# Swapping which engine reads a shared PSUM bank first: the bias addition of VectorE ahead of ScalarE's copy

## The chip, the cores and the metric

The kernel runs on one core of a Trainium2 chip. The metric is the device time of one launch in microseconds (us); three launches of the kernel before gave 3203.61, 3207.11 and 3209.1 us, so the median is 3207.11 us. A profile comes from one more execution of the same program, which took 3203.72 us.

## The reference

The input is 64 graphs of 256 nodes with 256 features each, and one sparse adjacency matrix `adj` (256 x 256) shared by all. Four layers follow each other. Layers 0, 1 and 3 have the same form, and layer 2 is an attention layer:

```python
# layers 0, 1, 3
pre_u = h @ W1[:256]                 # per node
pre_v = h @ W1[256:]
hidden = relu(pre_u[:, None] + pre_v[None, :] + b1)
S   = sigmoid(hidden @ W2 + b2)      # per pair of nodes
a_t = einsum('buv,bud->bvd', S * adj, h)
m_t = (adj^T h) * h
z   = beta1*h + beta2*(a_t @ Wa + ba) + beta3*(m_t @ Wm + bm)
# layer 2
feats = h @ W1^T;  f1 = feats @ W2 + b2
vals  = softmax(leaky_relu(f1[:,None] + f1[None,:]) + adj) @ feats
out   = vals + bias2 + h
```

`S` only matters where `adj` is not zero, and the kernel computes scores for those pairs of nodes (edges) alone.

## The kernel before

All data is fp32. Two graphs at a time (`g` = 0, 1) go through the four layers as one state, and two such states, side "a" and side "b", run interleaved: while one state is in its score stage (`scores`, L768 on, the heavy part), the other does the light parts of its layers. Sixteen rounds of this cover the 64 graphs.

The order of instructions on TensorE, VectorE and ScalarE is written out by hand. `PLAN` (L65) holds one string of letters for each combination of layer and side; `beside` (L919) advances one generator per letter: `T` makes the scores of one block of edges (two selecting matmuls into a PSUM tile of pool `ga`, then two VectorE passes with accumulated sums), `F`, `O` and `R` do the same for edges that were gathered, for the diagonal and for the left-over edges, `L` and `N` advance the light state, and `E` and `Z` turn the sums into scores (`rated_all`, L791). All three engines take their instructions strictly in the order recorded. DMA queues of SyncE (SP) and GpSimd (POOL) are not part of that order; a scheduler places them by when their inputs are ready.

The function around the change is `before` (L726), a light part that runs at the start of layers 0, 1 and 3. For each half `m` of the nodes and each graph `g` (four times per layer) it does this:

- two accumulating matmuls write one PSUM tile `t` of 128 x 512 fp32: columns 0 to 255 are `pre_u` of 128 nodes and columns 256 to 511 are `pre_v`. The tile fills one bank. It comes from pool `ps`, which has four buffers.
- L748: ScalarE copies the first half of the bank to the SBUF tile `puv`.
- L749: VectorE adds the bias row `b1row` to the second half and writes it to `puv`.
- The two instructions read different halves of one bank. The framework orders any two engines that touch one bank, so the second of them in program order waits for the first.
- after the second graph of a half, two SP DMAs (L753) write `puv` to two tables in DRAM, `tableu` (ScalarE's half) and `tablev` (VectorE's half); `fetch` (L847) then gathers rows from them by indirect DMAs that POOL issues (L861).
- ScalarE rounds `puv` to the two `part` tiles (L762, two casts), and VectorE subtracts to get the remainders (L765). The `T` blocks of the next score stage read the parts.

`puv` has a single buffer, used by both states in turn. Copy and addition stand as pairs 384 times in a run.

Other ScalarE work that stands in its queue around these pairs, and that the prediction follows: `hwa` (L391, a copy that empties a `ga` tile), `h` (L462, a copy of transposed features), `hT` (L520 on), and in `rated_all` (L791 on) two activations that make `val` (tanh, then add 1). VectorE follows `val` with three tiny instructions on `wt` (L797 to L799) and with the product `rm` (L804), which TensorE multiplies with `gu`. `mT` (L378) is a VectorE product that TensorE needs for `Wm`. In layer 2 the pair `e` and `f` (L496, L499) already reads one bank with VectorE first and ScalarE second. Since helper `Noting` (L96) records every operation of the three engines, the profile puts them all on L104; the tiles' names tell them apart.

Of the kernel before, what the change touches and what calls it, by code (L numbers as in the profile page):

```python
# [12 lines left out]
ALU = mybir.AluOpType  # L13
# [33 lines left out]
def fetches_of(l):  # L47

    def part(b, x):
        y = 1 - x if places(b)[0] > places(b)[1] else x  # L50
        return b, x, y

    first, then = [], [(None, 0, 0)]
    for b in FETCHED[l]:
        one = [part(b, x) for x in range(2)]
        (first if min(places(b)) == 0 else then).append(one[0])
        (first if max(places(b)) == 0 else then).append(one[1])
    by = lambda p: p[1]
    first.sort(key=by)
    waiting = [p for p in then if p[0] and p[1] and min(places(p[0])) == 0]  # L60
    last = sorted((p for p in then if p[0] and p not in waiting), key=by)
    return [first, then[:1] + waiting + [(None, 1, 1)] + last]
# [25 lines left out]
def blk(c):  # L88
    return slice(c * P, (c + 1) * P)
# [37 lines left out]
def adj_seq_kernel(ctx: ExitStack, tc: tile.TileContext, a: dict, out: bass.AP):  # L127
# [15 lines left out]
    tensor, vector, scalar = Noting(nc.tensor), Noting(nc.vector), Noting(nc.scalar)  # L143
# [35 lines left out]
    w1, wa, wm, b1row, w2row, zbias = {}, {}, {}, {}, {}, {}  # L179
# [372 lines left out]
    def few(stack):  # L552
# [173 lines left out]
        def before(st, l):  # L726

            hT = st["hT"]
            st["puv"] = puv = one.tile([P, 2, 2, 2, D], FP, tag="puv", name="puv")
            st["parts"] = parts = [one.tile([P, 2, 2, 2 * D], FR, tag=f"part{k}" + st["side"], name=f"part{k}") for k in range(2)]  # L730
            order = [(m, g) for m in range(2) for g in range(2)]
            if l == LAST:
                order = [(m, g) for g in range(2) for m in range(2)]

            st["tables"] = [
                tables.tile([N, 2 * D], FP, tag="table" + t + st["side"], name="table" + t) for t in "uv"
            ]

            st["fetches"] = []
            st["fetched"] = {b: got_.tile([P, 2, D], FP, tag="fetched", name="fetched") for b in FETCHED[l]}  # L740
            st["left"] = one.tile([P, D], FP, tag="left" + st["side"], name="left")
            for m, g in order:
                if l == LAST and (m, g) == (1, 0):
                    st["flip"](1)
                t = psum()
                for c in range(2):
                    mm(out=t, lhsT=hT[:, c, g, blk(m)], rhs=w1[l][:, c], start=c == 0, stop=c == 1)
                scalar.copy(puv[:, m, 0, g, :], t[:, 0, :])  # L748
                vector.tensor_tensor(puv[:, m, 1, g, :], t[:, 1, :], b1row[l], ALU.add)  # L749
                if g == 1:  # L750
                    x = puv[:, m].rearrange("p w g d -> p (w g d)")
                    for w, rows in enumerate(st["tables"]):
                        nc.sync.dma_start(out=rows[blk(m)], in_=x[:, w * 2 * D : w * 2 * D + 2 * D])  # L753
                    st["fetches"] += fetches_of(l)[m]
                    if numbered:
                        fetch(st)
                    elif st not in unfetched:
                        unfetched.append(st)
                    yield
                    flat = [p[:, m].rearrange("p w d -> p (w d)") for p in parts]  # L760
                    for k, h in enumerate(halves):
                        scalar.copy(flat[k][h], x[h])  # L762
                    yield
                    for k, h in enumerate(halves):
                        vector.tensor_tensor(flat[k][halves[1 - k]], x[h], flat[k][h], ALU.subtract)  # L765
                yield
# [80 lines left out]
        def fetch(st):  # L847

            now, st["fetches"] = st["fetches"], []
            for block, x, y in now:  # L850
                rows, ids = st["tables"][y], (ids_u, ids_v)[y]
                if block is None:
                    to, ids = st["left"], (left_u, left_v)[x]
                    rows = rows.rearrange("n (g d) -> (n g) d", g=2)
                else:
                    f = SOME.index(block)
                    to, ids = st["fetched"][block].rearrange("p g d -> p (g d)"), ids[:, f : f + 1]
                    if places(block)[y] == 0:
                        rows = rows[blk(0)]
                with tc.issue_after(fetches[-1]) if fetches else nullcontext():  # L860
                    this = nc.gpsimd.indirect_dma_start(  # L861
                        out=to, out_offset=None, in_=rows, in_offset=bass.IndirectOffsetOnAxis(ap=ids, axis=0),
                        compute_op=(ALU.bypass, ALU.add)[x],
                    )
                fetches.append(this.ins)
# [26 lines left out]
        def stream(side, starts):  # L892

            sts = [{"b": b, "side": side} for b in starts]
            if side == "a":
                sts[0]["hT"] = hT0
            load(sts[0])
            short = dict(L=before(sts[0], GNN[0]))
            kind = None
            for i, st in enumerate(sts):  # L900
                yield short, kind, (st, GNN[0])
                yield dict(L=steps(after(st, GNN[0]), before(st, GNN[1])), N=turns(st)), (GNN[0], side), (st, GNN[1])
                yield dict(L=steps(after(st, GNN[1]), attention(st), before(st, GNN[2]))), (GNN[1], side), (st, GNN[2])
                short, kind = dict(L=after(st, GNN[2])), None
                if i + 1 < len(sts):
                    load(sts[i + 1])
                    short, kind = dict(L=after(st, GNN[2]), N=before(sts[i + 1], GNN[0])), (LAST, side)
            yield short, None, None
# [151 lines left out]
```

## Time and profile before

| | before |
|---|---|
| median of three launches | 3207.11 us (3203.61 to 3209.1) |
| profiled execution, device time | 3203.72 us |
| its span, first to last instruction | 3202.0 us |
| granted TensorE clock | 0.995 |
| one copy of the first half (ScalarE) | 372 ns, 384 times |
| one bias addition of the second half (VectorE) | 420 ns, 384 times |
| one cast to a part (ScalarE) | 1044 ns, 384 times |
| one subtraction (VectorE) | 1221 ns, 384 times |
| one `T` pass over 128 x 256 (VectorE) | 418 ns, 1920 times |

The span is the time from the first to the last instruction on the core; the device time is 1.7 us longer. "Busy" is the time in which an engine executes. A group of instructions is named by its output and inputs, `out<-in`, with partitions x elements; after the bar come its total time, the mean of one and the idle time of the engine right before such instructions, with what ended it after `<-`. In a timeline each row gives the start, the duration, the engine and the instruction, `xN` for N in a row, and in brackets the idle time before it. PE is TensorE, PEld its weight loads, DVE VectorE, ACT ScalarE.

### The profile page before, as it was taken

How to read it: one execution, taken by the hardware profiler on the slowest of the kernel's cores; microseconds unless marked ns; L12 is line 12 of the kernel's file. 1: busy time of each engine (PE TensorE's matmuls, PEld its weight loads, DVE VectorE, ACT ScalarE, POOL GpSimd, SP SyncE). 2: the span in 40 equal slices, each digit the busy share in tenths (PEclk: the TensorE clock that was granted, in tenths of full speed). 3: DMA queues.
4: the chain of work that ended last, by engine and by line, in shares of the span. 5: the costliest groups of instructions: out<-in, count | busy, mean ns of one | idle time of the engine just before them, and what ended most of it. 6: DMA issues, size and time to landing. Idle time of an engine off the chain costs nothing.

```text
span 3202.0 us, 48626 instructions
## 1 busy us (share of the span) xinstructions
PE 3117.7 (97%) x14648; PEld 2228.7 (70%) x14648; DVE 2913.5 (91%) x10312; ACT 1358.9 (42%) x2658; POOL 1875.4 (59%) x1371
## 2 busy tenths in 40 slices
PE   7999999999999999999999999999999999999998
PEld 4667777677767667676777776767767676676766
DVE  7989999898999989999899998989989899898998
ACT  3444444434344443434444444444443434434343
POOL 2747566564656647556475564756657465564754
PEclk8999999999999999999999999999999999999999
DMA  5757576675756758577576665757667576675755
GB/s 154 155 127 183 133 180 136 146 172 127 187 132 163 162 119 190 139 162 161 128 182 133 169 155 134 179 128 178 137 144 170 128 183 133 158 162 118 191 130 111
DMA packets 231726, 486.59 MB, mean 152 GB/s; under 512 B 30880, under 2 KB 48160, under 8 KB 231456
## 3 DMA queue, kind: packets, MB, share of 16 engines
q0 software_dynamic: 147456, 327.24, 51.8%
q1 hardware_dynamic: 82416, 154.96, 13.6%
q8 instruction: 119, 1.95, 0.3%
q10 hardware_dynamic: 1584, 1.20, 0.1%
q14 instruction: 151, 1.24, 0.1%
HBM read 365.84 MB, written 117.44 MB: 151 GB/s over the span
## 4 chain that ended last, share of the span: by engine, by line
PE 68%; DVE 17%; issue 4%; ACT 3%; DMA 3%; POOL 2%; DVEq 0%; POOLq 0%; ACTq 0%
PE ps L104 44%; PE ga L104 24%; DVE junk L104 6%; DVE part L104 5%; POOL fetched L861 2%; DVE rm L104 2%; DMA fetched<-tablev,ids_v 1%; DMA left<-tablev,left_v 1%; ACT logits L104 1%; ACT ro L104 1%; DVE e L104 1%; DVE mT L104 1%; DVE own L104 1%; DVE logits L104 1%; DVE puv L104 0%
## 5 line engine op out<-in xcount | busy, mean ns | idle before, releaser
L861 POOL DMA_INDIRECT fetched<-tableu,ids_u x576 | 739.0, 1283 | 880.8 <-DVE junk L104 272.9
L861 POOL DMA_INDIRECT fetched<-tablev,ids_v x576 | 877.1, 1523 | 333.8 <-DMA fetched<-tableu,ids_u 182.3
L104 PE MATMUL ps<-L_gnn_w,hT 128*128 128x512 f32 x1536 | 718.2, 599 | 9.4 <-issue 5.4
L104 DVE SCALAR_TENSOR_TENSOR junk<-ga,L_gnn_w2row 128x256 f32<-128x256 f32 x1920 | 713.8, 418 | 4.4 <-PE ga L104 1.5
L104 PE MATMUL ga<-part,pick_u 128*128 128x512 f32 x960 | 519.8, 542 | 6.0 <-DVE mT L104 3.3
L104 DVE TENSOR_TENSOR part<-puv,part 64x1024 fp32r<-64x1024 f32 x384 | 468.8, 1221 | 11.8
L104 ACT CAST part<-puv 64x1024 fp32r<-64x1024 f32 x384 | 401.0, 1044 | 164.6 <-DVE puv L104 155.5
L104 PEld LDWEIGHTS ps<-L_gnn_w,hT 128*128 128x128 f32 x1536 | 286.6, 191 | 263.2 <-issue 222.2
L104 DVE SCALAR_TENSOR_TENSOR junk<-fetched,L_gnn_w2row 128x256 f32<-128x256 f32 x1152 | 432.2, 420 | 17.7 <-DMA fetched<-tablev,ids_v 13.4
L104 PE MATMUL ga<-part,pick_v 128*128 128x512 f32 x960 | 380.0, 396 | 0.5 <-issue 0.4
L104 PE MATMUL ga<-L_gnn_Wa,hT 128*128 128x256 f32 x1536 | 366.5, 382 | 1.8 <-DVE junk L104 1.8
L104 PE MATMUL ga<-adj,h 128*128 128x256 f32 x1536 | 361.8, 380 | 0.1
L104 ACT COPY puv<-ps 128x256 f32<-128x256 f32 x384 | 139.7, 372 | 520.2 <-PE ps L104 394.6
L104 PEld LDWEIGHTS ga<-adj,h 128*128 128x128 f32 x1536 | 292.6, 191 | 75.8 <-issue 37.8
L104 PEld LDWEIGHTS ga<-L_gnn_Wa,hT 128*128 128x128 f32 x1536 | 291.5, 192 | 62.6 <-issue 23.3
L104 DVE TENSOR_TENSOR puv<-ps,L_gnn_b1row 128x256 f32<-128x256 f32 x384 | 156.2, 420 | 136.2 <-ACT puv L104 134.7
L104 PE MATMUL ps<-sa,hwa 128*128 128x256 f32 x1024 | 239.5, 382 | 2.2 <-DVE sa L104 1.7
L104 DVE TENSOR_TENSOR rm<-gva,val 128x1024 f32<-128x1024 f32 x192 | 234.6, 1222 | 3.5 <-ACT val L104 0.6
L104 PEld LDWEIGHTS ga<-part,pick_u 128*128 128x128 f32 x960 | 182.3, 190 | 78.1 <-issue 35.7
L104 PE MATMUL ps<-mT,L_gnn_Wm 128*128 128x512 f32 x512 | 235.9, 593 | 0.0
L104 ACT ACTIVATE ro<-gvo,wt 64x256 fp32r<-64x256 f32 x384 | 194.4, 506 | 90.6 <-DVE wt L104 66.7
L104 PEld LDWEIGHTS ga<-part,pick_v 128*128 128x128 f32 x960 | 182.2, 190 | 68.4 <-issue 42.8
(152 smaller groups left out, 4293.4 us busy)
## 6 DMA issues: line engine op xcount, KB each, us to landing
tableu<-puv SPq DMA_DIRECT2D x192, 256.0 KB
tablev<-puv SPq DMA_DIRECT2D x192, 256.0 KB
hT<-in_xT_dram SPq DMA_DIRECT2D x32, 512.0 KB
h<-in_x_dram SPq DMA_DIRECT2D x64, 256.0 KB
out_dram<-h SPq DMA_DIRECT2D x64, 256.0 KB
fetched<-tableu,ids_u POOLq DMA_INDIRECT x576
fetched<-tablev,ids_v POOLq DMA_INDIRECT x576
L_gnn_w<-in_L_gnn_W_dram SPq DMA_DIRECT2D x6, 256.0 KB
```

Source lines behind the costliest of these rows:

```text
L104: self.last = getattr(self.engine, op)(*a, **k)
L861: this = nc.gpsimd.indirect_dma_start(out=to, out_offset=None, in_=rows, in_offset=bass.IndirectOffsetOnAxis(ap=ids, axis=0), compute_op=( ...
```

## The change

Two lines of `before` change places. No operand, size or engine changes.

```diff
                 for c in range(2):
                     mm(out=t, lhsT=hT[:, c, g, blk(m)], rhs=w1[l][:, c], start=c == 0, stop=c == 1)
+                vector.tensor_tensor(puv[:, m, 1, g, :], t[:, 1, :], b1row[l], ALU.add)
                 scalar.copy(puv[:, m, 0, g, :], t[:, 0, :])
-                vector.tensor_tensor(puv[:, m, 1, g, :], t[:, 1, :], b1row[l], ALU.add)
                 if g == 1:
```

In the built program the sequence of instructions on TensorE, VectorE, ScalarE and POOL is the same before and after. What differs is the waits: the 384 additions wait for TensorE in place of ScalarE, and the 384 copies wait for VectorE in place of TensorE. The bank is released to TensorE by the copy rather than by the addition. On SP's queue the write of `tablev` now mostly stands ahead of that of `tableu`.

## The prediction

> **What bounds the kernel now.** I read the page's busy times first, then busy time by stretch, then the waits, then the timeline of ScalarE and VectorE around single pairs.
>
> ```profile
> PE 3117.7 (97%) x14648; PEld 2228.7 (70%) x14648; DVE 2913.5 (91%) x10312; ACT 1358.9 (42%) x2658; POOL 1875.4 (59%) x1371
> PE 68%; DVE 17%; issue 4%; ACT 3%; DMA 3%; POOL 2%; DVEq 0%; POOLq 0%; ACTq 0%
> ```
>
> TensorE looks like the bound, VectorE close behind, ScalarE far from it. The pattern repeats every 196 us, sixteen times, with 24 pairs each. I use the cycle from 1020 to 1216 us and split it by stretch (columns: length; busy PE, PEld, DVE, ACT, POOL; clock; DMA share; GB/s):
>
> ```profile
> 1020.00:1149.00 129.00, 128.14 (x606) 92.70 (x605) 125.00 (x456) 57.03 (x112) 82.15 (x60) 1.00 0.72 163
> 1149.00:1155.50 6.50, 6.50 (x23) 3.81 (x22) 2.33 (x9) 2.74 (x5) 0.00 (x0) 1.00 0.26 82
> ```
>
> VectorE is busy for 125.0 of 129 us in the long stretch: nothing that delays it there has room. In the short one (and its twin, 1190 to 1195.5 us, with 1.51 of 5.5) TensorE alone is the bound. Who waits at the pairs of this cycle:
>
> ```profile
> DVE puv L104 <- ACT puv L104: 8.1, 7, 1.7
> ```
>
> VectorE waits for the copy 7 times, 8.1 us. The other 17 pairs have VectorE arriving late, with the copy long done. This is the point: the change helps the 7 and hits ScalarE's queue in the 17.
>
> **The change part by part.** No instruction is added or removed. A copy will start about 0.03 us after the addition ends (today the addition starts 33 ns after the copy at the earliest, and in layer 2 `f` 33 ns after `e`), and all that stands behind the copy on ScalarE waits with it. Two places in the cycle have work behind it that VectorE needs at once. First place, ScalarE, then VectorE:
>
> ```profile
> 1054.17 0.37 ACT L104 COPY puv<-ps 128x256 f32<-128x256 f32 x1
> 1054.78 0.59 ACT L104 COPY hwa<-ga 128x512 f32<-128x512 f32 x1 [0.23 <-PE ga L104]
> 1056.49 0.37 ACT L104 COPY puv<-ps 128x256 f32<-128x256 f32 x1 [1.13 <-PE ps L104]
> 1056.89 0.31 ACT L104 ACTIVATE val<-raw,L_gnn_halfb 128x21 f32<-128x21 f32 x1
> 1057.24 0.22 ACT L104 ACTIVATE val<-val 128x21 f32<-128x21 f32 x1
> ```
>
> ```profile
> 1057.72 0.74 DVE L104 TENSOR_TENSOR puv<-ps,L_gnn_b1row 128x256 f32<-128x256 f32 x2
> 1058.39 0.14 DVE L104 TENSOR_TENSOR wt<-val,awo 128x1 f32<-128x1 f32 x1
> ```
>
> VectorE adds for both pairs at 1057.72 and takes `wt` next, which needs `val`. Today `val` is done at 1057.46, because ScalarE ran ahead. After the change the first copy can start only at 1058.17 (first addition's end 1058.14 + 0.03); behind it stand `hwa` 0.59, the second copy 0.37, `val` 0.31 and 0.22. With 0.03 to 0.04 between them: 1058.54, 1059.16, 1059.56, 1059.90, 1060.15. So `wt` starts at 1060.18, not 1058.39: VectorE stands for **1.8 us**. TensorE's first `Wm` matmul at 1061.14 needs `mT`, which ends at 1060.65 today; about 0.5 of the 1.8 is hidden there, and no longer at 1067.82, where `rm` had ended only 0.14 before its matmul.
>
> Second place, again ScalarE, then VectorE, then TensorE's loads:
>
> ```profile
> 1112.71 0.37 ACT L104 COPY puv<-ps 128x256 f32<-128x256 f32 x1
> 1113.10 0.31 ACT L104 ACTIVATE val<-raw,L_gnn_halfb 128x21 f32<-128x21 f32 x1
> ...
> 1117.37 0.35 ACT L104 COPY puv<-ps 128x256 f32<-128x256 f32 x1
> 1117.62 0.58 ACT L104 COPY h<-ps 128x512 f32<-128x512 f32 x1
> 1118.54 2.11 ACT L104 CAST part<-puv 64x1024 fp32r<-64x1024 f32 x2 [0.34 <-issue]
> ```
>
> ```profile
> 1114.87 0.42 DVE L104 TENSOR_TENSOR puv<-ps,L_gnn_b1row 128x256 f32<-128x256 f32 x1
> 1115.21 0.15 DVE L104 TENSOR_TENSOR wt<-val,awo 128x1 f32<-128x1 f32 x1
> ...
> 1118.09 0.42 DVE L104 TENSOR_TENSOR puv<-ps,L_gnn_b1row 128x256 f32<-128x256 f32 x1
> ...
> 1119.91 2.47 DVE L104 TENSOR_TENSOR part<-puv,part 64x1024 fp32r<-64x1024 f32 x2
> 1122.41 1.23 DVE L104 TENSOR_TENSOR rm<-gva,val 128x1024 f32<-128x1024 f32 x1
> ```
>
> ```profile
> 1123.69 0.20 PEld L104 LDWEIGHTS ps<-rm,gu 128*64 128x64 f32 x4 [0.19 <-DVE rm L104]
> ```
>
> The addition ends at 1115.29; copy, `val` and its second step (0.37 + 0.31 + 0.22 and four gaps) end at 1116.29, so `wt` moves from 1115.21 to 1116.32: **1.1 us**. The next addition ends at 1118.51; the copy 0.35 and `h` 0.58 now stand between it and the casts, which start about 0.86 later. The first cast then ends at 1120.45, VectorE's subtraction waits 0.57, and `rm` waits another 0.25 for its `val` (ended at 1122.34, now 0.86 later): **0.8 us**. `rm` ends at 1123.64 and TensorE loads from it at 1123.69, so these 1.9 us reach TensorE whole.
>
> Small terms. Two pairs (1020.80, 1089.76) put the copy between the addition and the casts; casts 0.4 later, of which the subtraction's slack leaves 0.2 each; VectorE's idle 0.39 at 1099.0 can take one: +0.2. At 1020.94 TensorE waits for a bank that the copy would release 0.4 later; that is hidden by what VectorE loses next: 0, or 0.4 if not. `tableu` is issued behind the copy, 0.4 later at 1154 and 1194.8, and POOL's gathers start on it; VectorE's 0.25 wait for a gathered block at 1209.6 grows: 0 to 0.4, I take 0.2, the middle. Later `hT` copies (0.5) fit into 0.9 us of slack before TensorE needs them: 0.
>
> Gains. Of the 7 waits, five stand where VectorE next waits for TensorE anyway; they give nothing. At 1081.42 the wait of 0.28 goes and at 1194.84 the addition starts 0.41 earlier, but the casts start no earlier, which leaves about 0.2 each: -0.4. VectorE's arrival bounds them: 0 to -0.7.
>
> **Sum.** 1.8 + 1.1 + 0.8 + 0.2 + 0.2 - 0.4 = 3.7 us a cycle. I count 15 cycles, since the first starts up by another plan and the last runs thin: +56 us. The profiled execution took 3203.72, so 3259.5; the median of the runs lies 3.4 above it: **3263 us**, 1.7% slower. Ends: the 1.1 and 0.8 alone, 1.9 x 15 = 28, 3235; all losses without gains, and the bank's and POOL's 0.4 in full, 1.8 + 1.1 + 0.8 + 0.4 + 0.4 + 0.4 = 4.9, x 16 = 78, 3285.
>
> One rule is weighed here. PE is at 97%, and read so, VectorE's stalls would be hidden and the sum 0. The Trainium skill ("Perfetto Trace Analysis", Identifying the Most-Contended Engine) says that matmul busy time is no good measure of TensorE's headroom and that weight-load busy time is the better one; that is 70% here, and by it the stalls count. The load at 1123.69, waiting 0.19 for `rm`, agrees with the rule.
>
> **The rivals.** *Faster.* ScalarE is 42% busy, so its queue might take the delay while VectorE keeps its gains. For it: 134.7 us of VectorE's idle time stand under this wait. Against: most of a 1.3 or 1.7 wait is TensorE's matmul, and only the copy's 0.41 can go, 7 x 0.41 x 16 = 46 (3161) if every one reached the end; the two that can give (0.28 + 0.41) x 16 = 11: 3196. It decides if VectorE's first use of `val` comes over 1.8 us after the additions rather than directly behind them. *Same.* TensorE, 97% busy, sets the end and VectorE's 3.7 us fit in its idle stretches (4.2 and 4.0 us a cycle): 3207. Against: the `rm` load, and TensorE, once late, is fully busy in just those stretches. A change that does nothing would also end here; the changed waits speak against that. *Much slower.* TensorE meets banks that ScalarE frees microseconds later, at several tiles per cycle: 3290 to 3320. Against: except at 1020.94 the next use of such a bank comes 1.5 us or more after the addition.
>
> **How the numbers follow.** A measurement can tell about 0.2% (6.4 us) from no change. My case, 3214 to 3288: 0.70; much slower, above: 0.07; same: 0.10; faster: 0.13. Slower is 0.77. The range 3203 to 3288 takes in the main case and about half of "same"; 3235 and 3285 lie in it.
>
> **What would show it.** Right: the wait of the addition for the copy is gone; `wt` waits for `val` (almost nothing today) for about 2.9 us a cycle, some 45 in all; the copy waits for the addition for hundreds of us; the subtraction waits for the casts; TensorE waits more for `rm` and `mT`. Wrong: `wt` idle stays small, or it grows and TensorE's idle does not; then VectorE had room that I did not see.

## The result and the profile after

The kernel after takes 3324.57 us (median of four launches, 3321.38 to 3327.45); before, timed beside it, took 3208.11. The ratio is 1.0368, with a 95% interval of 1.0354 to 1.0382. That is 116 us slower, where 56 were predicted: the sign and the stalls that the prediction named were right, but they are half of the loss, and the time lies above the range. The profiled execution took 3323.97 us, its span is 3322.3 us, and the granted clock was 0.99 (0.995 before). That is 0.5% less, which by an estimate from these two numbers could make at most 17 of the 116 us even if all of the time followed the clock.

Busy times and the chain that ended last, from the page of after:

```profile
PE 3146.9 (95%) x14648; PEld 2234.6 (67%) x14648; DVE 2915.5 (88%) x10312; ACT 1359.8 (41%) x2658; POOL 1873.6 (56%) x1371
DVE 33%; PE 30%; DMA 9%; issue 9%; ACT 9%; POOL 8%; DVEq 0%; POOLq 0%; SPq 0%; ACTq 0%
```

Busy times moved little; shares fell because the span grew. The chain of work changed: TensorE's share went from 68% to 30%, VectorE's doubled, and DMA and GpSimd rose from 5% together to 17%. The change touches no transfer except for the order of the two table writes on SyncE's queue, so that is the first hint of a cost that the prediction does not hold.

The waits of after (who waited for whom: total us, times, longest):

```profile
ACT puv L104 <- DVE puv L104: 841.2, 321, 10.4
DVE junk L104 <- DMA left<-tablev,left_v: 55.0, 33, 3.3
DVE wt L104 <- ACT val L104: 38.5, 31, 1.5
DVE junk L104 <- DMA fetched<-tablev,ids_v: 32.5, 33, 2.0
PE ps L104 <- DVE mT L104: 38.1, 30, 2.8
PE ps L104 <- ACT puv L104: 18.8, 16, 5.0
```

Three waits of before to set beside them, the first with the engines the other way round:

```profile
DVE puv L104 <- ACT puv L104: 134.7, 121, 1.7
DVE junk L104 <- DMA left<-tablev,left_v: 8.3, 12, 1.4
DVE junk L104 <- DMA fetched<-tablev,ids_v: 13.4, 24, 1.7
```

The first row is the change itself: the copy now stands behind the addition. The third is the predicted stall (some 45 us predicted). The second and fourth are new in size: before, VectorE waited 8.3 us for `left` and 13.4 us for `fetched`, both gathered by GpSimd. VectorE's whole idle time rose from 285 to 403 us: `wt` +38.5, `left` +46, `fetched` +20, `part` +21, less 14 at the addition itself. TensorE's idle time rose from 80 to 171 us. The sixth row is the bank that the copy now releases; the prediction put it at 0, or at 0.4 us a cycle if it was not hidden.

The places that the prediction priced. First place in after, ScalarE, then VectorE:

```profile
1100.51 0.37 ACT L104 COPY puv<-ps 128x256 f32<-128x256 f32 x1 [3.54 <-DVE puv L104]
1100.78 0.59 ACT L104 COPY hwa<-ga 128x512 f32<-128x512 f32 x1
1101.26 0.39 ACT L104 COPY puv<-ps 128x256 f32<-128x256 f32 x1
...
1102.02 0.22 ACT L104 ACTIVATE val<-val 128x21 f32<-128x21 f32 x1
```

```profile
1100.06 0.75 DVE L104 TENSOR_TENSOR puv<-ps,L_gnn_b1row 128x256 f32<-128x256 f32 x2
1102.28 0.16 DVE L104 TENSOR_TENSOR wt<-val,awo 128x1 f32<-128x1 f32 x1 [1.47 <-ACT val L104]
```

Just as foreseen, copy, `hwa` and copy run in front of `val`, and `wt` stands for 1.47 us (1.8 predicted). Most of the difference is visible in the first fence: `hwa` starts 0.27 us after a copy of 0.37 us, and the next copy 0.48 us after an `hwa` of 0.59 us. These rows overlap by 0.1 us each, and the prediction added whole durations and a gap. From the start of the first copy to `wt` it is 1.77 us, where the prediction had 2.01. Second and third place in after:

```profile
1162.58 0.16 DVE L104 TENSOR_TENSOR wt<-val,awo 128x1 f32<-128x1 f32 x1 [1.03 <-ACT val L104]
...
1167.88 2.54 DVE L104 TENSOR_TENSOR part<-puv,part 64x1024 fp32r<-64x1024 f32 x2 [0.62 <-ACT part L104]
1170.63 1.22 DVE L104 TENSOR_TENSOR rm<-gva,val 128x1024 f32<-128x1024 f32 x1 [0.21 <-ACT val L104]
```

They stall 1.03 (1.1 predicted), 0.62 (0.57) and 0.21 (0.25). The three places together lose 3.3 us a cycle, against 3.7.

The part that the prediction missed is seen on another path. SyncE's queue, GpSimd and VectorE, in before (pair 9 of the cycle, counted from 0: second graph of the first half, state a, layer 1):

```profile
1081.42 0.33 SPq L753 DMA_DIRECT2D tableu<-puv  x1
1081.88 0.41 SPq L753 DMA_DIRECT2D tablev<-puv  x1
...
1085.93 0.99 POOL L861 DMA_INDIRECT fetched<-tableu,ids_u  x1 [7.08 <-DVE wt L104]
...
1100.67 1.54 POOL L861 DMA_INDIRECT left<-tablev,left_v  x1 [0.30 <-issue]
...
1105.25 0.43 DVE L104 SCALAR_TENSOR_TENSOR junk<-left,L_gnn_w2row 128x256 f32<-128x256 f32 x1 [0.25 <-DMA left<-tablev,left_v]
```

And the same pair in after, where VectorE's addition starts at 1124.98 (1081.42 before):

```profile
1125.42 0.33 SPq L753 DMA_DIRECT2D tablev<-puv  x1
1125.85 0.37 SPq L753 DMA_DIRECT2D tableu<-puv  x1
...
1131.48 1.16 POOL L861 DMA_INDIRECT fetched<-tableu,ids_u  x1 [5.69 <-DVE junk L104]
...
1146.64 1.54 POOL L861 DMA_INDIRECT left<-tablev,left_v  x1 [0.30 <-issue]
...
1151.81 0.43 DVE L104 SCALAR_TENSOR_TENSOR junk<-left,L_gnn_w2row 128x256 f32<-128x256 f32 x1 [3.32 <-DMA left<-tablev,left_v]
```

Between the first and the last GpSimd row shown stand eight more gathers, each starting 0.30 us after the end of the one before it. This string takes 16.3 us before and 16.7 after (to the end of `left<-tablev`), so it is as long as its gathers and has no slack; a start that comes later moves its end by as much. From the start of the addition to the first gather it is 4.51 us before and 6.50 after; to VectorE's use of `left`, 23.83 and 26.83. Of these 3.0 us more, 2.0 are the later start, 0.4 the string and 0.6 the landing of its last gather. The wait for `left` grew from 0.25 to 3.32 us: they went whole into VectorE's idle time.

Why does the first gather come later? It reads `tableu`, ScalarE's half. The VectorE instruction named in the brackets of its row (`wt` before, `junk` after) makes nothing that the gather reads. The last semaphore update of the write to `tableu` stands in the trace at 1085.18 before and at 1130.72 after, and the gather starts 0.75 us later both times: it waits for the table. The 2.0 us are 0.87 of later issue, counted from the start of the addition, and 1.11 by which the write takes longer (3.76 us from issue to landing before, 4.87 after).

Before, the copy ran ahead of VectorE wherever VectorE came late, so `tableu` was issued before the addition ended. Medians over 13 cycles, in us after the addition's end:

| | pair 5 | pair 9 | pair 11 |
|---|---|---|---|
| before: `tableu` issued | -1.20 | -0.43 | -0.65 |
| before: first gather of the batch | 2.08 | 2.74 | 5.51 |
| after: `tableu` issued | 0.44 | 0.45 | 0.44 |
| after: first gather of the batch | 5.99 | 5.88 | 7.10 |

`tableu` is issued 0.9 to 1.6 us later here (0.9 to 2.4 at all twelve pairs of a cycle that start a batch), and besides it stands behind `tablev` on SyncE's queue. The page of after gives a median of 2.7 us from issue to landing for `tablev` and 4.2 for `tableu`, but it has a landing for only 81 and 16 of the 192 writes; by the last semaphore update of nearly every write the medians are 3.3 and 4.0.

The three pairs of the table are among those that lose most. Over all twelve the first gather moves by -0.6 to 4.8 us. In five of them (5, 9, 13, 18 and 22) it starts 0.75 to 1.0 us after the landing of `tableu`, before and after alike (medians); in the other seven it is 1.3 us and more, so there something else mostly holds it back.

### The profile page after: what moved, and what is told of

Same layout as the page of the kernel before. It is cut to its first block, busy times and chain, and to the rows that moved or that the text cites. A ratio compares the mean times of both kernels' runs of the same rounds, so it can differ in the third digit from the quotient of the medians.

```text
span 3322.3 us, 48614 instructions
## 1 busy us (share of the span) xinstructions
PE 3146.9 (95%) x14648; PEld 2234.6 (67%) x14648; DVE 2915.5 (88%) x10312; ACT 1359.8 (41%) x2658; POOL 1873.6 (56%) x1371
## 4 chain that ended last, share of the span: by engine, by line
DVE 33%; PE 30%; DMA 9%; issue 9%; ACT 9%; POOL 8%; DVEq 0%; POOLq 0%; SPq 0%; ACTq 0%
PE ps L104 21%; DVE junk L104 12%; PE ga L104 9%; DVE part L104 8%; POOL fetched L861 6%; DMA fetched<-tablev,ids_v 5%; DVE rm L104 3%; DMA left<-tablev,left_v 3%; ACT part L104 2%; DVE puv L104 2%; DVE own L104 2%; POOL left L861 2%; DVE mT L104 1%; ACT puv L104 1%; DMA fetched<-tableu,ids_u 1%
## 5 line engine op out<-in xcount | busy, mean ns | idle before, releaser
L104 PE MATMUL ps<-L_gnn_w,hT 128*128 128x512 f32 x1536 | 719.3, 599 | 24.1 <-ACT puv L104 18.8
L104 DVE TENSOR_TENSOR part<-puv,part 64x1024 fp32r<-64x1024 f32 x384 | 469.5, 1223 | 32.8 <-ACT part L104 17.2
L104 PE MATMUL ps<-mT,L_gnn_Wm 128*128 128x512 f32 x512 | 249.9, 622 | 44.1 <-DVE mT L104 37.7
L104 PE MATMUL ps<-rm,gu 128*64 128x128 f32 x3072 | 203.0, 278 | 24.8 <-DVE rm L104 23.5
```

Source lines behind the costliest of these rows:

```text
L104: self.last = getattr(self.engine, op)(*a, **k)
```

## The experiments

Theory 1 is the prediction's: the copy waits, and what stands behind it on ScalarE reaches VectorE and TensorE late. Theory 2 is new: the later write of `tableu` moves the string of gathers. Eleven kernels tell them apart. Each ratio is to runs of before beside it, whose median was 3205.93 (e1 to e4), 3211.01 (e5 to e8) or 3208.36 us (e9 to e11); "excess" is (ratio - 1) x 3208 us. The last two columns are VectorE's idle time in us.

| | time, us | ratio (95% interval) | excess, us | idle before `wt` | idle before `left` |
|---|---|---|---|---|---|
| before | 3208.11 | 1 | 0 | 0.5 | 9.7 |
| after | 3324.57 | 1.0368 (1.0354 to 1.0382) | 118 | 39.0 | 55.5 |
| e1, add first, u half | 3271.01 | 1.0199 (1.0182 to 1.0216) | 64 | 39.0 | 17.9 |
| e2, copy first, v half | 3262.07 | 1.0177 (1.0160 to 1.0194) | 57 | 0.5 | 58.3 |
| e3, after, four pairs back | 3282.52 | 1.0241 (1.0224 to 1.0258) | 77 | 0.5 | 63.8 |
| e4, after in layer 3 only | 3239.29 | 1.0099 (1.0082 to 1.0116) | 32 | 0.5 | 33.9 |
| e5, after, `tableu` first on SP | 3294.68 | 1.0257 (1.0239 to 1.0274) | 82 | 39.0 | 31.5 |
| e6, before, `tableu` last on SP | 3277.72 | 1.0206 (1.0189 to 1.0223) | 66 | 0.5 | 67.0 |
| e7, after, v gathered first | 3268.36 | 1.0181 (1.0164 to 1.0199) | 58 | 39.0 | 19.6 |
| e8, u half, six pairs of layer 3 | 3201.79 | 0.9970 (0.9960 to 0.9980) | -10 | 0.5 | 19.1 |
| e9, u half, all but four pairs | 3235.53 | 1.0079 (1.0058 to 1.0099) | 25 | 0.5 | 35.6 |
| e10, u half, four pairs alone | 3266.14 | 1.0176 (1.0156 to 1.0196) | 56 | 39.2 | 12.0 |
| e11, e8 and one pair more | 3202.53 | 0.9975 (0.9963 to 0.9986) | -8 | 0.5 | 16.0 |

**e1 and e2: one half of the effect each.** In e1 VectorE still goes first, but on the u half, so ScalarE waits and `tableu` is the earlier table. In e2 ScalarE goes first, but on the v half, so nobody new waits and `tableu` is the later table.

```diff
# e1, against after
-vector.tensor_tensor(puv[:, m, 1, g, :], t[:, 1, :], b1row[l], ALU.add)
-scalar.copy(puv[:, m, 0, g, :], t[:, 0, :])
+vector.tensor_tensor(puv[:, m, 0, g, :], t[:, 0, :], b1row[l], ALU.add)
+scalar.copy(puv[:, m, 1, g, :], t[:, 1, :])
# e2, against after
+scalar.copy(puv[:, m, 1, g, :], t[:, 1, :])
+vector.tensor_tensor(puv[:, m, 0, g, :], t[:, 0, :], b1row[l], ALU.add)
```

> VectorE still adds first and ScalarE copies second, but the halves change places: VectorE adds the bias to the pre_u half (tableu is then written by the first instruction), ScalarE copies the pre_v half. The result is the same sum, since the bias may be added to either half. Theory 1 (of the 117 us, about half is ScalarE's queue behind the copy and half is tableu landing late, on which every batch of gathers starts): tableu is early again, the gathers come in time, VectorE's waits for gathered blocks fall back from 93 us to about 30, time 3255 to 3275. Rival (all is ScalarE's queue, the late gathers only follow from it): no change against the changed kernel, 3310 to 3330.

> The order of before (ScalarE copies first, VectorE adds second) with the halves exchanged: ScalarE copies pre_v, VectorE adds the bias to pre_u, so that tableu alone is written late and nothing changes in ScalarE's queue. Theory 1: late tableu costs by itself, 3235 to 3270. Rival (ScalarE's queue alone): 3202 to 3214, as before.

Both times came within the bounds of what these expectations and those of e3 and e4 call theory 1, the two causes together (VectorE's waits for gathered blocks are 38.6 us in e1, about 30 expected). The idle times split: `wt` waits in e1 alone, `left` waits for most in e2 alone. 64 + 57 = 121 us, and both together, the kernel after, lose 118: two costs of nearly one size. That the sum comes out so closely is partly luck, since costs don't add up further below (e9 and e10), and e1 holds a little of the second cost too: it issues `tableu` 0.03 us after the addition's end, before it was 0.73 us ahead of it (median).

**e3 and e4: where in the cycle.** e3 puts four pairs back to copy first (state b, second half of the nodes, layers 0 and 1: the places priced in the prediction). e4 has the order of after in layer 3 alone.

```diff
# e3, in after: copy first where this holds, else add first
+if st["side"] == "b" and m == 1 and l != LAST:
# e4: copy first where this holds, else add first
+if l != LAST:
```

> As the changed kernel, but the four pairs of a cycle with val, h or hwa behind the copy (layers 0 and 1 of side b, second half of the nodes) keep the old order. Theory 1: the waits of wt, rm and the subtraction there go (38.5 + about 15 us of VectorE's idle time), late tableu stays for the rest: 3255 to 3275. Rival (the four pairs are all of it): 3202 to 3220. Rival (they are not on the path): 3315 to 3330.

> Addition first only in layer 3, where VectorE waited for the copy in six of eight pairs; layers 0 and 1 keep the old order. Theory 1: nothing in ScalarE's queue hurts here, but tableu is late in this layer: the two gather waits of the changed kernel's cycle (1.28 and 1.02 us) remain, 16 x 2 = 32 us less some gain: 3225 to 3240. Rival (queue alone): VectorE's gains show, 3195 to 3208.

e3 removed the wait of `wt` (39.0 to 0.5 us) but won back 41 us only and missed its expected range (3282.52, expected 3255 to 3275). The idle time before `left` rose from 55.5 to 63.8, which I read as VectorE, now earlier, meeting the same late gathers. e4 came as expected: 32 us in a layer in which none of the prediction's three places lies. The idle time before `left` is 33.9 us there.

**e5 and e6: SyncE's queue alone.** No engine's order changes; only the two table writes are held in one order.

```diff
-for w, rows in enumerate(st["tables"]):
-    nc.sync.dma_start(out=rows[blk(m)], in_=x[:, w * 2 * D : w * 2 * D + 2 * D])
+for w in (0, 1):                  # e5, in after; e6: (1, 0) in before
+    with tc.issue_after(one_.ins) if w == 1 else nullcontext():    # e6: w == 0
+        one_ = nc.sync.dma_start(out=st["tables"][w][blk(m)], in_=x[:, w * 2 * D : w * 2 * D + 2 * D])
```

> The kernel after, but SyncE's two table writes are held in the order of before: tableu, then tablev. TensorE, VectorE, ScalarE and GpSimd are as in the kernel after, which took 3324.57 us. In after, tableu is issued 0.44 us after the addition's end and lands 4.2 us later, behind tablev (2.7 us). Theory 2a (half of the unforeseen 56 us is the place behind tablev in the queue): tableu lands some 1.5 us sooner, the first gather of a batch starts 1 us sooner or more, and the time falls to 3275 to 3300 us; VectorE's idle time before junk<-left falls from 55.5 us to under 35. Rival 2b (it is only that the copy, and with it the issue of tableu, comes 0.9 to 2.4 us later than before; the queue's order adds nothing): 3312 to 3330 us, idle time before junk<-left above 45 us.

> The kernel before, but SyncE's two table writes are held in the order of after: tablev, then tableu. Nothing else changes on any engine; copies and additions stand as in before (3207.11 us). tableu is then issued about 0.03 to 0.4 us after the addition's end in place of 0.4 to 2.0 us before it, and queues behind tablev. Theory 2 (a late tableu alone, without any wait of ScalarE, costs what copy-first with the halves exchanged cost, 56 us): 3245 to 3275 us, VectorE's idle time before junk<-left rises from 9.7 us to 40 or more, no idle time before wt. Rival (the 56 us came from the exchange of the halves between the engines, not from the table): 3200 to 3215 us.

e6 is the cleanest run of the case. Its waits:

```profile
DVE puv L104 <- ACT puv L104: 134.0, 114, 2.3
DVE junk L104 <- DMA left<-tablev,left_v: 66.5, 33, 4.1
```

VectorE waits for the copy as before (134.7 there), nothing waits for `val`, and still the kernel loses 66 us, a little more than the expected bound of 3275: the later table by itself is the unforeseen cost. e5 shows that in after the queue's order makes a part of it: `tableu` first brings back 118 - 82 = 36 us, and the idle time before `left` falls to 31.5. What remains over e1 is 18 us. e5 issues `tableu` 0.43 us after the addition's end and `tablev` 0.84, e1 0.03 and 0.44; that this later issue of both makes the 18 us is not shown by itself.

**e7: start each batch with the table that is early.** In after, all blocks take their row of `tablev` first and add that of `tableu`.

```diff
-        y = 1 - x if places(b)[0] > places(b)[1] else x
+        y = 1 - x
-    first, then = [], [(None, 0, 0)]
+    first, then = [], [(None, 0, 1)]
-    return [first, then[:1] + waiting + [(None, 1, 1)] + last]
+    return [first, then[:1] + waiting + [(None, 1, 0)] + last]
-                    to, ids = st["left"], (left_u, left_v)[x]
+                    to, ids = st["left"], (left_u, left_v)[y]
```

> The kernel after, but every gathered block takes its row of tablev first and adds that of tableu, so each batch of gathers on GpSimd starts with tablev, which VectorE's addition, now first, has made. Sizes and numbers of gathers stay. This is the mirror of the run in which VectorE added the bias to the u half first. Theory 2 (of the 117 us, some 50 come from the batch's first gather waiting for the later of two tables): 3262 to 3282 us, idle time before junk<-left near 18 us, before wt still near 39 us. Rival (the loss does not hang on which table the batch starts with): 3312 to 3330 us.

```profile
DVE wt L104 <- ACT val L104: 38.5, 31, 1.5
DVE junk L104 <- DMA left<-tableu,left_u: 19.1, 24, 1.5
DVE junk L104 <- DMA fetched<-tableu,ids_u: 17.6, 26, 3.8
```

As expected, 60 of the 118 us are gone without any change to copy or addition, and the wait of `wt` is untouched. What is left, 58 us, is close to what the prediction put on the waiting copy. TensorE's wait for the bank (the sixth row of after's waits) falls from 18.8 to 6.4 us here, although every copy still comes second: two thirds of it went away with the late gathers and were no cost of the bank by itself.

**e9 and e10: the predicted places by themselves.** e10 is before with the u half added first in the four pairs only; e9 has it everywhere else.

```diff
# e10; e9 has: not (...)
+if st["side"] == "b" and m == 1 and l != LAST:
+    vector.tensor_tensor(puv[:, m, 0, g, :], t[:, 0, :], b1row[l], ALU.add)
+    scalar.copy(puv[:, m, 1, g, :], t[:, 1, :])
+else:
     scalar.copy(puv[:, m, 0, g, :], t[:, 0, :])
     vector.tensor_tensor(puv[:, m, 1, g, :], t[:, 1, :], b1row[l], ALU.add)
```

> VectorE adds the bias to the u half first everywhere, except in the four pairs of a cycle that the prediction priced (state b, second half of the nodes, layers 0 and 1), where ScalarE copies the u half first as in before. With all pairs exchanged this form took 3271 us, 65 over before. Theory (the prediction's terms 1.8, 1.1 and 0.8, at those four pairs, are most of the 65): 3205 to 3232 us, VectorE's idle time before wt back under 2 us. Rival (the 65 is spread over the other 20 pairs, tables and banks): 3240 to 3262 us, although wt no longer waits.

> The counterpart: the kernel before, with the bias added to the u half first only in the four pairs of a cycle that the prediction priced. Theory: the three terms 1.8 + 1.1 + 0.8 = 3.7 us a cycle, times 15, are 56 us, less what VectorE can regain: 3245 to 3265 us, wt waits near 38 us. Rival (TensorE hides a part, and the 65 us of all pairs came mostly from elsewhere): 3212 to 3235 us.

e10 loses 56 us, the prediction's 3.7 x 15 = 56 for its three places (its median lies 1 us over the expected bound). The match to the microsecond is partly luck: at 3.3 us a cycle the three places make 50 us, and VectorE's waits for gathered blocks grow by 6 us besides. e9 fell between the two expectations: 25 us that none of the three terms holds, with 35.6 us of idle time before `left`. The two add up to 82, but all pairs together (e1) lose 64. The stalls overlap: idle time before `left` is 35.6 in e9 and 17.9 in e1. The likely reason is that a VectorE that stood for `wt` comes to the gathered rows later and waits less there; no run shows it by itself.

**e8 and e11: add first only where VectorE waited.** In layer 3 VectorE waited for the copy in six pairs of a cycle (0.27 to 1.73 us each), with no `val` close behind.

```diff
# e8, in before, with the body of e10; e11 adds: or (l == GNN[1] and st["side"] == "a" and (m, g) == (0, 1))
+if l == LAST and (m, g) != (1, 1):
```

> The kernel before, but in layer 3, in three of the four pairs of each state, VectorE adds the bias to the u half first and ScalarE copies the v half second. These are six of the eight pairs of a cycle in which VectorE waited for the copy in before (0.27 to 1.73 us idle each); no val or wt stands close behind them, and tableu is written no more than 0.1 us later than before. Theory: the gain that the prediction allowed, 0 to 0.7 us a cycle, without its losses: 3194 to 3209 us, probably not to be told from before. Rival (each copy held behind an addition costs by itself, through later banks and casts): 3215 to 3240 us.

> The run with VectorE first on the u half in three of four pairs of layer 3 (0.997 of before, 9 us faster), with one pair more: state a, layer 1, first half of the nodes, second graph, where VectorE waited 0.28 us for the copy. Theory (what VectorE gains where it waited reaches the end): 0.28 x 15 = 4 us at most on top: 3192 to 3203 us, or 0.995 to 0.998 of before. Rival (the casts behind it and the table take it back): 3203 to 3212 us, 0.998 to 1.001 of before.

e8 is 0.30% faster than before, 10 us (interval 6 to 13), more clearly than I expected, and with e11 the only version in the case that beats both kernels (e11 can't be told from e8, so the seventh pair stays undecided). VectorE's wait for the copy is nearly gone:

```profile
DVE puv L104 <- ACT puv L104: 7.3, 19, 1.3
```

It was 134.7 us. As the prediction said, most of it was TensorE's matmul and became a wait for that (113.5 us); and 9 us came back as idle time before `left`. Where the 10 us come from the profiles don't show: VectorE's idle time falls from 285.2 to 282.9 us, TensorE's from 80.2 to 78.7, and the two profiled executions differ by 4 us only. Beside e4, which has the v half added first in all pairs of layer 3 and loses 32 us, e8 shows again that the half matters more than the order.

## Why the prediction was right in sign and half in size

- *What bounds the kernel.* Right. At 97% busy, TensorE still had no cover for VectorE's stalls: in e10 VectorE stands 38.7 us longer before `wt`, TensorE's idle time grows from 80 to 129 us, and the kernel loses 56. The Trainium skill ("Perfetto Trace Analysis", Identifying the Most-Contended Engine) says that matmul busy time is not a good measure of how close TensorE is to its limit, and this case agrees.
- *1.8 + 1.1 + 0.8 at three places.* Right: 1.47, 1.03 and 0.83 as idle times in after, and 56 us in e10. Each term is within 0.35 us; the first was too high mostly by the overlap of rows on ScalarE, which its own rows show in the second place (`h` starts at 1117.62, the copy before it ends at 1117.72).
- *Small terms: casts 0.2.* Too low but small: VectorE waits 17.2 us for ScalarE's parts in e1, after and e7 alike (17.1 to 17.2), about 1.1 us a cycle, of which 0.62 is the third place.
- *`tableu`: 0 to 0.4, I take 0.2.* **This is the step that failed.** It priced two issues per cycle, 0.4 us later each, and one wait of 0.25. e6 measured the term by itself: 66 us, or 4.1 us a cycle. Three things were missing. First, where VectorE comes late to the bank, the copy, and with it the issue of `tableu`, had run ahead by up to 2 us; the prediction used exactly this head start for `val`, and did not apply it to the DMA behind the same copy. Second, `tableu` also moves behind `tablev` on SyncE's queue: the section on the change states the new order, and the prediction never priced it. Third, I bounded the price by the 0.4 us of one copy and read it at two places, while all twelve batches of a cycle start on `tableu`, five of them within 1 us of its landing, and the string of gathers behind it has no slack where VectorE reads its end.
- *The bank at 1020.94: 0, or 0.4 if not.* Too low: 18.8 us of waits in after, 1.2 us a cycle. Most of it goes away when the gathers come in time (6.4 us in e7).
- *Gains -0.4 a cycle, 0 to -0.7.* The size is in the range, but by luck: the places were wrong. Five of e8's six pairs are those that the prediction put at nothing, and only the sixth (1194.84) was to give 0.2 a cycle, 3 us in all; e8 gains 10 us (6 to 13), 0.6 a cycle. The pair at 1081.42, put at another 0.2, is the one that e11 adds, and nothing more is seen there. That gains could be had alone the prediction did not look for.
- *Rivals.* "Same" and "faster" fell by the chain of waits and the times. "Much slower", 3290 to 3320, came nearest in time, though by its own mechanism it is wrong: TensorE waits 18.8 us for such banks, against 118 us lost. A rival that follows DMA behind the moved instruction was missing, and the range ended at 3288 because of that.

What stays open: how the 66 us of e6 divide between the later issue and the place in the queue. At the source the trace shows two delays of one size: at pairs 5, 9, 13, 18 and 22, e6 issues `tableu` 1.03 us later than before, and the write takes 0.96 us longer (3.65 us against 2.69, means over 13 cycles). Not all of the second is the place: in after, where the write takes 3.61, holding `tableu` first (e5) brings it to 3.10. In after the place makes 36 of some 60 us; a run that delays the issue alone in before was not made.

## What to carry to other kernels

If an instruction is moved back, follow every consumer of its output, the DMAs issued behind it first, and measure its head start over the other engine in the trace of before: what is lost is that head start (up to 2 us here), not the duration of the instruction in front (0.4), and a write that falls behind another on its queue loses more (0.5 us here: 3.6 us from issue to landing in after against 3.1 in e5, means of the five pairs named above). A string of transfers with equal small gaps has no slack, so what it loses at its start it loses at its end (2.0 and 2.4 us in the string above); look there for a short wait (0.25 us here) that tells that the margin is already used up. And where one order helps some places and hurts others, choose it place by place: add first on the u half gained 10 us in six pairs of a cycle, and lost 64 in all 24.

## What the runs showed of the hardware beyond that

- Two writes of 256 KB each, issued 0.4 us apart on SyncE's queue, don't land alike: `tablev`, in front, 3.3 us after its issue and `tableu` 4.0 (medians over 191 and 192 writes of after, by their last semaphore updates). With `tableu` held in front (e5) it takes 3.7 and `tablev` 4.0; with a head start of 0.5 us and more for `tableu` in most pairs (e8), 2.3 and 3.9.
- A gather that waits for a table starts 0.75 us after the last semaphore update of the table's write (0.75 to 0.76 us in all 13 cycles at pairs 9, 13 and 22, before and after).
- An indirect gather occupies GpSimd for 0.95 to 1.9 us in the string of after between 1131.48 and 1148.18, and the next one starts 0.30 us after its end. The rows don't show when the data is there: `left<-tablev` is issued at 1146.64 and its row ends at 1148.18, but its last semaphore update stands at 1151.72, and VectorE goes on at 1151.81, 5.17 us after the issue (the median to landing is 4.5 us for `left<-tablev` by the page of after). The Trainium skill ("Perfetto Trace Analysis", DMA Instruction — SWDGE (GPSIMD)) says that such a row ends with the last descriptor and not with the last byte; this case agrees.
- A row on ScalarE can start 0.1 us before the row ahead ends (1100.78, where the copy ahead runs from 1100.51 for 0.37 us). The two `val` rows behind it (1101.67 for 0.32 us, then 1102.02) don't overlap.
